# At most three gathers in flight: a wait on the third gather ahead, in a graph attention kernel

## The chip, the core and the metric

The kernel runs on one core of a Trainium2 chip. The metric is the device time of one execution in microseconds. The kernel before took 2567.61 us (median of three runs, 2564.39 to 2570.67). An execution under the hardware profiler is slower: the profiled span is 3156.3 us. Times of single instructions and of waits below come from that profiled execution; the metric is always the time without the profiler.

## The reference

A graph of 3327 nodes has 256 features for each node and a random adjacency matrix in which about 0.48% of the entries are set, some 16 neighbours for each node. Layer 0 is an attention layer in which the score of a neighbour does not depend on the receiving node. Layers 1 to 3 are transformer layers whose attention runs over the neighbours alone:

```
qkv = layer_norm(x, g1, be1) @ w_qkv          # 8 heads of 32
scores = einsum('nhd,mhd->hnm', q, k) * SCALE
scores = where(adj != 0, scores, -inf)
attn = softmax(scores, axis=-1)
out = einsum('hnm,mhd->nhd', attn, v).reshape(n, 256)
x = x + out @ w_proj + b_proj
h2 = layer_norm(x, g2, be2)
x = x + gelu(h2 @ w1 + b1) @ w2 + b2          # 256 -> 1024 -> 256
```

## The kernel before

The first part (up to about 505 us of the profiled span) reads the adjacency matrix, computes layer 0, and turns each row of the matrix into a list of neighbours. The nodes are ranked by their number of neighbours, so that blocks of 128 nodes (there are 26) hold nodes with similar counts. `CAPS` gives the number of neighbour slots of each block, 40 for the first and 10 for the last, 448 in all.

Layers 1 to 3 are run by the class `Layer`. Keys and values of all nodes lie in HBM, one row of 512 floats (528 in layer 1) for each node, in `kv[L]`. For each block and each of its slots, one indirect DMA issued by GpSimd gathers 128 such rows, one for each node of the block, into SBUF: 128 rows of 2 KB, 256 KB for a gather, 448 gathers for a layer, 1344 in all. `issue` (L1288) issues the gathers of one group of up to four slots (`GS = 4`) into one tile of a ring of ten (`NBUF = 10`); the gather itself is L1303. At the start of a layer ten groups are issued; after that one more group is issued each time `values` has read a group and so freed a ring tile. Layer 1 also issues row gathers of `t1` (L1263), and the last layer scatters output rows (L1505), on the same GpSimd queue.

`scores` (L1313) multiplies the keys of a group by the block's queries (L1325) and sums over each head (L1326) on VectorE. After the last group of a block `softmax` runs; some turns later `values` (L1355) weights the values (L1366, VectorE) and adds them up on TensorE with transposes into PSUM (L1372). Projection, layer norm, the feed-forward part and the next layer's q, k and v are cut into small steps, which `some` puts between the groups: matmuls at L1396, L1439, L1462 and L1492, activations at L1445. The keys and values for the next layer are written to HBM by L1500. A layer's gathers need all of these rows, so layers do not overlap in their gathers.

The order on every engine is the order of the calls in the program; a framework layer adds the semaphores. Each DMA that GpSimd issues belongs to one of eight lanes in turn, with a semaphore for each lane, and a DMA waits until the one before it on its lane, which is the eighth ahead, has landed. That is the limit of eight of which the change speaks. The first gather of a group also waits until VectorE (and in layer 1 ScalarE) has read what the ring tile held before.

Of the kernel before, what the change touches and what calls it, by code (L numbers as in the profile page):

```python
# [60 lines left out]
CB = 4  # L61

FAR = 2.0 ** 100


@with_exitstack
# [457 lines left out]
def sparse_path(ctx, tc, ins, out, dram, flag):  # L524
    nc = tc.nc
# [40 lines left out]
    class Norm:  # L566


        def __init__(self, n, name):
            self.n, self.name = n, name  # L570
            self.mv = small.tile([P, 4, 2], FP, tag="mv", name=f"mv_{name}")
# [690 lines left out]
    def gather_rows(b):  # L1262
        nc.gpsimd.indirect_dma_start(  # L1263
            out=t2[:, b, :], out_offset=None, in_=t1,
            in_offset=bass.IndirectOffsetOnAxis(ap=perm[:, b:b + 1].bitcast(U32), axis=0))
# [11 lines left out]
    class Layer:  # L1277
        def __init__(self, L, w, nxt):
            self.L, self.w, self.nxt = L, w, nxt
            self.groups = [g for b in ORDER for g in slots[b]]  # L1280
            self.issued = 0
            self.tiles, self.sc, self.wp, self.q, self.po = {}, {}, {}, {}, {}
            self.rows = 0

            self.short, self.long = [], []
            self.rate = self.credit = 0.0

        def issue(self):  # L1288

            if self.issued == len(self.groups):  # L1290
                return
            L, W = self.L, KVW[self.L]
            b, s0 = self.groups[self.issued]
            self.issued += 1
            while L == 1 and self.rows < min(NB, ORDER.index(b) + 3):
                gather_rows(ORDER[self.rows])
                self.rows += 1
            n = min(GS, CAPS[b] - s0)
            t = ring.tile([P, GS * KVW[1]], FP, tag="kv", name=f"kv_{L}_{b}_{s0}")
            t = t[:, :GS * W].rearrange("p (s c) -> p s c", c=W)  # L1300
            for s in range(n):
                k = 2 * D + s0 + s
                nc.gpsimd.indirect_dma_start(  # L1303
                    out=t[:, s, :], out_offset=None, in_=kv[L],
                    in_offset=bass.IndirectOffsetOnAxis(ap=t2[:, b, k:k + 1].bitcast(U32), axis=0))
            self.tiles[b, s0] = t


# [4 lines left out]
        def scores(self, b, s0):  # L1313
# [4 lines left out]
            if s0 == 0:  # L1318
                self.sc[b] = work.tile([P, LMAX, HEADS], FP, tag="sc", name=f"sc_{L}_{b}")
                if L == 1:  # L1320
                    nc.vector.tensor_scalar(pad[b],
                                            t2[:, b, 2 * D:2 * D + S].bitcast(I32),
                                            0.0, FAR, ALU.is_equal, ALU.mult)
            k = t[:, :n, :D]
# [6 lines left out]
        def softmax(self, b):  # L1331
# [5 lines left out]
            nc.vector.tensor_tensor_reduce(  # L1337
                sc, sc, pad[b][:, :, None].to_broadcast([P, S, HEADS]), 1.0, FAR,
                ALU.add, ALU.min, mx)
# [294 lines left out]
```

## Time and profile before

| | |
|---|---|
| timed, median of three | 2567.61 us |
| profiled span | 3156.3 us |
| VectorE busy | 1935.3 us |
| TensorE matmul busy | 1794.0 us |
| GpSimd busy | 1362.7 us |
| ScalarE busy | 774.6 us |
| gathers, L1303 | 1344, mean 947 ns on GpSimd, 1273.0 us busy |
| data moved by GpSimd's DMAs | 370.26 MB |
| first and last gather start | 509.5 and 3068.0 us |

A line of the profile's groups reads: source line, engine, operation, what is written from what is read, count, then the busy time and the mean of one in ns, then the engine's idle time just before and what ended most of it. "issue" means that the profile shows nothing for which the engine waited; "remote" or "an unknown queue" that what ended the wait is not known. An engine's queue is shown with a q (POOLq is the queue of GpSimd): it decodes, holds waits and dispatches, and can run ahead of the engine. The time of a gather on GpSimd is the time in which its descriptors are made; the data arrive later, which is told by the lane's semaphore.

### The profile page before, as it was taken

To read this page: it belongs to the slowest core of one execution; us is meant where nothing else is said; L and a number is where in the kernel's file an instruction comes from. 1 tells how busy PE (TensorE), PEld (TensorE's weight loads), DVE (VectorE), ACT (ScalarE), POOL (GpSimd) and SP (SyncE) were. 2 spreads that over 40 slices of the span, in tenths; PEclk is the share of its full clock that TensorE was granted. 3 is DMA by queue.
4 is the path that set the end of the run, shared out by engine and by line. 5 is a ranking of instruction groups with operands and counts; after the bars stand their busy time and mean duration, and the time that the engine had idled before them with its cause. 6 is when DMAs were issued, how large, how long until landed. Compare 5 with 4: busy or idle time off the path is not lost.

```text
span 3156.3 us, 24036 instructions
## 1 busy us (share of the span) xinstructions
PE 1794.0 (57%) x7561; PEld 1163.5 (37%) x7561; DVE 1935.3 (61%) x3983; ACT 774.6 (25%) x1316; POOL 1362.7 (43%) x1458
## 2 busy tenths in 40 slices
PE   4767752255666666671457667666713435665556
PEld 3645531133333333350334333433512323433334
DVE  6688995457657656533656756755446556656554
ACT  4455621012222222230112212222300111212112
POOL 4000004545555554305555555544054555565550
PEclk9868766577787886785578778878755766776768
DMA  5334306645555565415455555555064554554560
GB/s 207 131 117 148 129 31 204 174 138 169 165 172 162 156 174 152 112 51 177 141 156 156 163 160 150 175 152 140 24 189 125 156 155 135 169 163 147 161 156 13
DMA packets 144486, 453.80 MB, mean 144 GB/s; under 512 B 29521, under 2 KB 40156, under 8 KB 141021
## 3 DMA queue, kind: packets, MB, share of 16 engines
q0 software_dynamic: 113056, 370.26, 40.9%
q1 hardware_dynamic: 9834, 53.90, 4.9%
q10 hardware_dynamic: 21458, 28.02, 2.5%
q8 instruction: 61, 1.00, 0.1%
q14 instruction: 77, 0.63, 0.1%
HBM read 420.64 MB, written 31.42 MB: 143 GB/s over the span
## 4 chain that ended last, share of the span: by engine, by line
DVE 25%; issue 18%; PE 18%; another core or an unknown queue 17%; POOL 11%; ACT 5%; DMA 5%; DVEq 0%; ACTq 0%; POOLq 0%; SPq 0%
POOL kv L1303 11%; DVE kv L1325 5%; DMA kv<-kv,t 4%; DVE sc L1326 3%; DVE vw L1366 3%; PE pu L1439 3%; PE po L1372 3%; PE py L1462 2%; DVE cand L735 2%; PE pk L1492 1%; PE s_pk L1010 1%; ACT s_aT L724 1%; DVE s_v L731 1%; PE pf L591 1%
## 5 line engine op out<-in xcount | busy, mean ns | idle before, releaser
L1303 POOL DMA_INDIRECT kv<-kv,t x1344 | 1273.0, 947 | 1210.3 <-issue 534.2
L1372 PE MATMUL po<-s_ident,vw 128*128 128x128 f32 x2688 | 475.4, 334 | 580.2 <-DVE vw L1366 387.2
L1372 PEld LDWEIGHTS po<-s_ident,vw 128*128 128x128 f32 x2688 | 395.5, 174 | 724.1 <-issue 373.5
L1325 DVE TENSOR_TENSOR kv<-kv,q 128x1024 f32<-128x1024 f32 (+3 forms) x363 | 413.1, 1138 | 397.1 <-ACT q L1311 274.6
L1366 DVE TENSOR_TENSOR vw<-kv,w 128x1024 f32<-128x1024 f32 x333 | 371.4, 1128 | 87.2 <-remote 84.6
L1326 DVE TENSOR_REDUCE sc<-kv 128x32 f32<-128x1024 f32 (+3 forms) x363 | 414.1, 1141 | 12.4
L1439 PE MATMUL pu<-fT,s_w 128*128 128x512 f32 (+3 forms) x768 | 341.2, 579 | 62.3 <-issue 35.8
L1462 PE MATMUL py<-gT,s_w 128*128 128x512 f32 (+2 forms) x672 | 321.8, 597 | 58.1 <-issue 50.2
L1400 DVE TENSOR_TENSOR t<-t,po 128x256 f32<-128x256 f32 x78 | 32.6, 418 | 390.8 <-remote 254.5
L1445 ACT ACTIVATE gT<-pu,pvb 128x512 f32<-128x512 f32 (+3 forms) x192 | 115.7, 607 | 628.2 <-remote 384.1
L1439 PEld LDWEIGHTS pu<-fT,s_w 128*128 128x128 f32 x768 | 157.4, 222 | 196.1 <-issue 146.4
L1462 PEld LDWEIGHTS py<-gT,s_w 128*128 128x128 f32 x672 | 132.6, 206 | 180.7 <-issue 144.0
L1396 PEld LDWEIGHTS po<-s_w_proj,oT 128*128 128x128 f32 x312 | 71.8, 255 | 281.8 <-issue 272.3
L1394 PE MATMUL po<-bias,s_ones_bf 96*128 96x256 bf16 x78 | 25.2, 324 | 259.7 <-issue 147.4
L1390 ACT COPY oT<-po 128x256 f32<-128x256 f32 x78 | 28.9, 371 | 548.5 <-remote 320.2
L711 POOL MEMSET s_abf<- 128x1 bf16 x23 | 2.2, 104 | 361.4 <-DVE s_v L731 253.7
L1492 PE MATMUL pk<-s_w_qkv,nT 128*128 128x512 f32 x208 | 128.4, 748 | 22.0 <-ACT nT L596 9.9
L735 DVE MAX8 cand<-s_v 128x8 f32<-128x208 bf16 x416 | 118.0, 360 | 0.9
L1396 PE MATMUL po<-s_w_proj,oT 128*128 128x256 f32 x312 | 113.1, 500 | 0.0
L723 PE MATMUL s_ptb<-s_ident_bf,s_abf 128*128 128x128 bf16 x676 | 67.1, 265 | 68.3 <-ACT s_abf L714 45.2
L591 PE MATMUL pf<-s_ident,xn_f 128*128 128x128 f32 x156 | 46.1, 444 | 86.8 <-ACT xn_f L588 66.7
L855 PE MATMUL s_pa<-s_aT,s_hs 128*128 128x256 bf16 x338 | 82.3, 290 | 13.2 <-DVE s_hs L817 13.2
(288 smaller groups left out, 2252.1 us busy)
## 6 DMA issues: line engine op xcount, KB each, us to landing
s_a<-in_adj_dram SPq DMA_DIRECT2D x25, 1663.5 KB
kv<-kv,t POOLq DMA_INDIRECT x1344
kv<-kvr ACTq DMA_DIRECT2D x52, 256.0 KB
kv<-s_kvr ACTq DMA_DIRECT2D x26, 256.0 KB
s_w<-in_L_gnn_w_dram SPq DMA_DIRECT2D x6, 1024.0 KB
t<-ql ACTq DMA_DIRECT2D x6, 592.0 KB
t<-s_x ACTq DMA_DIRECT2D x6, 512.0 KB
s_w_qkv<-in_L_gnn_w_qkv_dram SPq DMA_DIRECT2D x3, 768.0 KB
```

The lines of the kernel that those rows point to most:

```text
L735: nc.vector.max(out=self.cand[:, s, :], in_=self.v[:, s, :])
L855: nc.tensor.matmul(self.pa[:, c0:c0 + 2 * P], S.hs[:r, k, :P], aT[:r, k, :], start=(k == 0), stop=(k == NB - 1))
L1303: nc.gpsimd.indirect_dma_start(out=t[:, s, :], out_offset=None, in_=kv[L], in_offset=bass.IndirectOffsetOnAxis(ap=t2[:, b, k:k + 1].bitcas ...
L1325: nc.vector.tensor_mul(k, k, self.q[b][:, None, :].to_broadcast([P, n, D]))
L1326: nc.vector.tensor_reduce(self.sc[b][:, s0:s0 + n, :], k.rearrange("p s (h d) -> p s h d", d=HD), AX.X, ALU.add)
L1366: nc.vector.tensor_mul(vw[:, :n * D].rearrange("p (s h d) -> p s h d", h=HEADS, d=HD), v, self.wp[b][:, s0:s0 + n, :, None].to_broadcast([ ...
L1372: nc.tensor.matmul(self.po[b][:, k * P:(k + 1) * P], vw[:, at:at + P], ident, is_transpose=True, start=(s0 + s == 0 and k == 0), stop=(s0 ...
L1396: nc.tensor.matmul(ps, c["oT"][:, k * P:(k + 1) * P], w["w_proj"][:, k, :], start=False, stop=(k == 1))
L1439: nc.tensor.matmul(c["pu", f][:, :n], w["w1"][:, e, f * P:(f + 1) * P], c["hT"][:, e, :n], start=(e == 0), stop=(e == 1))
L1445: nc.scalar.activation(g[:, :n], c.pop(("pu", f))[:, :n], AF.Gelu_apprx_tanh, bias=w["b1"][:, f:f + 1])
L1462: nc.tensor.matmul(c["py"][e][:, :n], w["w2"][:, f, e * P:(e + 1) * P], g[:, :n], start=(f == 0), stop=last)
L1492: nc.tensor.matmul(ps[:, :c1 - c0], c["hT"][:, e, j * P:(j + 1) * P], nxt["w_qkv"][:, e, c0:c1], start=(e == 0), stop=(e == 1))
```

## The change

Each gather of a layer, from the fourth on, gets a dependence on the gather three ahead of it: it is not to be issued before that one has landed. The list `flight` holds the gathers of the layer; it is new for each layer, and row gathers and output stores are not in it. The purpose is to keep no more than three gathers in flight, where up to eight could be, so that the DMA engines hold less of a backlog when other transfers come. What is computed, and the order of the instructions, stays.

```diff
+FLIGHT = 3
+WAIT = mybir.DependencyInfo(mybir.DependencyClass.Sync, mybir.DependencyReason.DATA)
...
             self.issued = 0
+            self.flight = []
...
             for s in range(n):
                 k = 2 * D + s0 + s
-                nc.gpsimd.indirect_dma_start(
+                got = nc.gpsimd.indirect_dma_start(
                     out=t[:, s, :], out_offset=None, in_=kv[L],
                     in_offset=bass.IndirectOffsetOnAxis(ap=t2[:, b, k:k + 1].bitcast(U32), axis=0))
+
+                if len(self.flight) >= FLIGHT:
+                    tc.add_manual_dep(got.ins, self.flight[-FLIGHT].ins.name, WAIT,
+                                      reason="gathers in flight")
+                self.flight.append(got)
```

## The prediction

> **What bounds the kernel now.** I read the page first, then the rates of the stages (which engine is busy in which stretch), then the timeline and the chain of waits inside a stretch in which nothing disturbs the work. From the page:
>
> ```profile
> span 3156.3 us, 24036 instructions
> PE 1794.0 (57%) x7561; PEld 1163.5 (37%) x7561; DVE 1935.3 (61%) x3983; ACT 774.6 (25%) x1316; POOL 1362.7 (43%) x1458
> DVE 25%; issue 18%; PE 18%; another core or an unknown queue 17%; POOL 11%; ACT 5%; DMA 5%; DVEq 0%; ACTq 0%; POOLq 0%; SPq 0%
> L1303 POOL DMA_INDIRECT kv<-kv,t x1344 | 1273.0, 947 | 1210.3 <-issue 534.2
> ```
>
> No engine is full, and 17% of the chain, some 540 us, is put down to an unknown queue. The profiled execution takes 3156 us where the timed one takes 2567.61: about 590 us exist only under the profiler, nearly as many as those unexplained waits. So I don't take shares of this span as shares of the timed run; I look for a rate that explains the timed run.
>
> The stretches of the three layers, by the rates of the stages (us; PE, PEld, DVE, ACT, POOL busy; granted clock; DMA share, GB/s):
>
> ```profile
> 505.00:1310.00 805.00, 447.82 (x1580) 267.86 (x1580) 477.34 (x799) 167.52 (x378) 446.88 (x473) 0.73 0.58 168
> 1420.00:2170.00 750.00, 432.24 (x1550) 263.95 (x1549) 468.39 (x764) 157.22 (x266) 407.97 (x431) 0.74 0.53 158
> 2290.00:3070.00 780.00, 377.40 (x1395) 236.38 (x1394) 456.29 (x687) 126.42 (x203) 444.64 (x467) 0.69 0.54 156
> ```
>
> The timeline of GpSimd early in layer 2, where no ring slot is awaited yet:
>
> ```profile
> 1436.91 0.95 POOL L1303 DMA_INDIRECT kv<-kv,t  x1 [0.30 <-issue]
> 1438.16 0.95 POOL L1303 DMA_INDIRECT kv<-kv,t  x1 [0.30 <-issue]
> 1439.41 0.95 POOL L1303 DMA_INDIRECT kv<-kv,t  x1 [0.30 <-issue]
> ```
>
> A gather starts every 1.25 us (0.95 of work, 0.30 between two), never closer. The trace has 471, 448 and 467 GpSimd DMAs from the first gather of a layer to its last (layer 1 has row gathers among them, layer 3 the first output stores). At 1.251 us each that is 589 + 560 + 584 us. First gather of layer 1 at 509.5; 1310.8 to 1428.5 and 2190.8 to 2305.9 pass between layers; 88.3 follow the last gather. Sum: 509.5 + 589 + 117.7 + 560 + 115.1 + 584 + 88.3 = 2564 us, against 2567.61 timed. So the timed run looks like one in which GpSimd issues without a break, and the long idle times are the profiler's. VectorE, with at most 477 us busy in such a layer, keeps up with a group of four gathers each 5.0 us: at a layer's start it waits for landings ("DVE kv L1325 <- DMA kv<-kv,t", 17.7 us of the window from 1428 to 1480). The gathers' pace is the bound.
>
> The chain of waits in the same stretch (start, us, what):
>
> ```profile
> 1436.91 3.56 DMA kv<-kv,t
> 1440.47 0.02 issue
> 1440.49 0.04 POOLq L1303
> ...
> 1446.91 3.66 DMA kv<-kv,t
> 1450.57 0.02 issue
> 1450.59 0.04 POOLq L1303
> ```
>
> The gather that GpSimd started at 1436.91 landed at 1440.47, 3.56 us later, and that released GpSimd's queue, which held the wait of the eighth gather behind it (started 1446.91). So the queue runs some five gathers ahead of the engine, and the limit of eight costs the engine nothing.
>
> **What the Trainium skill says.** "DMA: Bandwidth & Descriptors", Anatomy of one DMA — SWDGE (gpsimd) path: a DMA from GpSimd costs about 2.0 us plus bytes over 436 GB/s, mostly waiting for the receipt of the last write, and a semaphore is waited for before dispatch, not by the DMA engines. For 256 KB that is an estimate of 2.6 us; with 0.95 of descriptor work ahead of it 3.55, and the trace has 3.56 to 3.72. "Perfetto Trace Analysis", DMA Instruction — SWDGE (GPSIMD): the profiled end is the end of descriptor generation, not the landing. The trace agrees: 0.95 us against a landing at 3.6. So the latency that counts here is not the 947 ns of the page. The first of these pages, Latency and other measured facts, gives HBM latency as 0.2 us on average and 2 us at high load: fewer transfers in flight could shorten each. No run here shows that yet.
>
> **The change part by part.** (1) Each of the 1344 gathers but the first three of a layer waits for the third ahead. In the built program the wait for its own lane (the eighth ahead) goes, the wait for a lane three back comes; PE, VectorE, ScalarE and SyncE keep their instructions and waits, and GpSimd gets 24 more instructions that only wait, near the row gathers and layer starts. The trace shows such a wait at 0.04 us: 24 × 0.04 = 1 us, nothing. (2) The limit itself. GpSimd's start of gather k must now follow landing(k-3) plus the time from a release to a start. That delay is in the trace: where VectorE freed a ring slot with GpSimd idle, the start came 0.26 us after (61 cases, median 0.259). The landing semaphores' increments are recorded in part; for the 115 gathers with all 16, start to last increment has quartiles of 3.48, 3.62 and 3.75 us. So the third ahead is ready at 3.62 + 0.26 = 3.88 us after its start, where it used to be given 3 × 1.251 = 3.75. The pace becomes 3.88 / 3 = 1.293 us, 0.042 more per gather: 1344 × 0.042 = 57 us. Behind the waiting gather on GpSimd stand only further gathers, the row gathers and stores; VectorE waits for them.
>
> That is the floor for these latencies, since a late landing delays a gather and an early one gives nothing back. I replayed the three layers with every gather's own landing time (last completion packet of the gather, shifted by 0.33 to meet the 16-increment ones), starts at the later of 1.251 after the previous and 0.26 after landing k-3: 176 us more. Of these some 40 come from bursts: at the start of layer 1 landings take 6 us and at the end of each layer they climb to 9 or 10, because there the DMA engines are full (0.9 busy at 1300 to 1322) and the backlog is the gathers' own; three in flight keep a full DMA engine just as full, so this part is not real. With landings cut off at 4.3 us the replay gives 136. If latencies are 0.1 us shorter in the timed run it is 103, with 0.2 shorter 72, with 0.33 shorter 47. I take 115, between the steady floor and the full replay. (3) The queue can't run five ahead any more; each dispatch waits on a landing. The 0.26 above contains this. (4) Gathers of rows and output stores wait for less than before: some 50 DMAs with 0 to 0.3 us, under 5 us, and not on the path.
>
> **The rivals.** A, the forecast: slower, 2567.6 + 115 = 2683; between +47 and +176 by the bounds above, so 2615 to 2744. B, nothing: the latency without the profiler is below 3.75 - 0.26 = 3.49 us. The skill's 2.6, if it already holds the descriptor work, would do it; then two landed gathers always wait and only rare late ones bind, 2567 to 2573. For it: even now two gathers or fewer are in flight at most starts (1226 of 1344 by the completion packets). Against it: every landing I followed in the chain in undisturbed stretches is 3.5 to 3.7. C, faster: fewer transfers in flight leave the engines to other traffic (instruction fetch, the rows written by L1500, weights), and the unexplained waits of 17% are partly real and shrink. If a tenth of the 540 us is real and half of it goes, 2567.6 - 27 = 2540. For it: PE, ScalarE and VectorE stall together beside dense gathers. Against it: the sum above leaves 3 us for such stalls in the timed run, and in most cases the limit changes nothing of what is in flight, only the timing. D, far slower: the whole 176 plus real bursts, 2760 or more, if a landing's release reaches GpSimd later than VectorE's does; with 0.40 for 0.26, (3.62 + 0.40) / 3 = 1.34, already a floor of 120 us.
>
> **How the numbers follow.** A 0.67, D 0.07, B 0.09, C 0.17. The predicted time is A's, 2683. The range has to take in B (from 2562) and A up to its top; D reaches a little into it: 2562 to 2765. Left out are most of C and a part of D, about 0.2. Faster 0.17, same within 0.2% (5 us) 0.09, slower 0.74.
>
> **What would show it.** In the changed profile gathers that follow each other without a ring wait should start 1.29 to 1.36 us apart, the gap before them 0.34 to 0.41 and no longer a constant 0.30; the idle time before L1303 should be put down to the landing of gathers rather than "issue"; landings should stay near 3.6 us. The 947 ns stay. The profiled span may rise less than the timed one, because there the ring is often full and hides the pace. I am wrong if the gap stays 0.30 (B), or if landings fall below 3.4 with fewer in flight, or if the stalls of PE and ScalarE shrink (C).

## The result, and the profile after

The changed kernel took 2750.85 us (2747.61 to 2752.35), the kernel before, run beside it on the same chip, 2566.99: a ratio of 1.071 (95% interval 1.070 to 1.073), 184 us slower. The forecast was 2683 with a range up to 2765. Its side and its mechanism hold; 68 us of the loss were missing from it. The measured time lies 7 us above the top of the forecast's own bounds (2744) and inside the stated range only because that reached further, towards rival D.

The page after. Its span, 2749.0 us, is now the same as the timed execution:

```profile
span 2749.0 us, 24060 instructions
PE 1696.8 (62%) x7561; PEld 1134.5 (41%) x7561; DVE 1942.6 (71%) x3983; ACT 781.8 (28%) x1316; POOL 1362.2 (50%) x1458
DVE 30%; DMA 25%; PE 19%; issue 11%; POOL 9%; ACT 4%; DVEq 0%; ACTq 0%; SPq 0%; POOLq 0%
L1307 POOL DMA_INDIRECT kv<-kv,t x1344 | 1272.4, 947 | 834.4 <-issue 266.0
kv<-kv,t POOLq DMA_INDIRECT x1344, 3.6
```

The work of a gather on GpSimd, 947 ns, is unchanged, and the busy times of VectorE and ScalarE are within 1% of those before.

The page ahead of the prediction is no fair basis for comparison: it was of a disturbed execution, and in a second profile of the kernel before its 590 us of stalls did not come again. So it doesn't hold either that an execution under the profiler is slower as such: this span, 2568.8 us, goes with a timed run of 2570.72. Page of the kernel before, second profile:

```profile
span 2568.8 us, 24036 instructions
DVE 14%; PE 13%; DMA 13%; POOL 9%; issue 8%; ACT 1%; DVEq 0%; POOLq 0%; SPq 0%; ACTq 0%
L1303 POOL DMA_INDIRECT kv<-kv,t x1344 | 1273.0, 947 | 643.7 <-issue 327.4
```

The shares of the chain that ended last (third line of the page after, second here) settle nothing. DMA has 25% after and had 5% in the first profile before, but here it has 13% of a chain that could be followed through 58% of the span only, and 20% with a limit of six, which costs no time (below). What can be compared are idle times and waits. GpSimd's idle time ahead of gathers rose from 643.7 to 834.4 us, that is by 191. Where it shows on VectorE is told by the waits, before (second profile) and after: engine and line that waited, for what, us in total, times, longest.

```profile
DVE kv L1325 <- DMA kv<-kv,t: 171.7, 105, 8.7
```

```profile
DVE kv L1334 <- DMA kv<-kv,t: 379.6, 180, 8.2
```

VectorE waits 208 us more for landings. It is a follower here: it waits because gathers start later. From the first gather's start of each layer to its last, before: 599.2, 587.6 and 611.0 us, after 678.3, 649.0 and 683.1: 212.6 more. Between the layers and after the last gather 31 us come back (265.4 to 234.2), and the first gather starts 1.2 earlier. 212.6 - 31.2 - 1.2 = 180.2, which is the difference of the two spans.

How the loss comes about is seen in GpSimd's timeline in layer 2 (start, us, what, idle time before it). First the kernel before, second profile, where the gather at 1411.22 is the first of its group and starts 1.25 us after the one ahead, like the others:

```profile
1407.47 0.94 POOL L1303 DMA_INDIRECT kv<-kv,t  x1 [0.30 <-issue]
1408.71 0.95 POOL L1303 DMA_INDIRECT kv<-kv,t  x1 [0.30 <-issue]
1409.96 0.95 POOL L1303 DMA_INDIRECT kv<-kv,t  x1 [0.30 <-issue]
1411.22 0.95 POOL L1303 DMA_INDIRECT kv<-kv,t  x1 [0.30 <-issue]
```

The changed kernel, where 1339.39 and 1344.89 are the first of their groups:

```profile
1339.39 0.94 POOL L1307 DMA_INDIRECT kv<-kv,t  x1 [0.76 <-DMA kv<-kv,t]
1340.64 0.95 POOL L1307 DMA_INDIRECT kv<-kv,t  x1 [0.30 <-issue]
1341.89 0.95 POOL L1307 DMA_INDIRECT kv<-kv,t  x1 [0.30 <-issue]
1343.14 0.95 POOL L1307 DMA_INDIRECT kv<-kv,t  x1 [0.30 <-DMA kv<-kv,t]
1344.89 0.94 POOL L1307 DMA_INDIRECT kv<-kv,t  x1 [0.80 <-DMA kv<-kv,t]
```

and in its chain of waits in the same stretch:

```profile
1340.64 3.51 DMA kv<-kv,t
1344.15 0.02 issue
1344.17 0.02 POOLq L1307
1344.19 0.70 issue
1344.89 3.48 DMA kv<-kv,t
1348.37 0.27 issue
1348.64 0.94 POOL kv L1307
1349.59 0.70 issue
1350.28 3.45 DMA kv<-kv,t
```

Three gathers of four still start 1.25 us after the one ahead of them; the delay falls on one in four. The gather at 1344.89 is the first of a group. The third ahead of it, started at 1340.64, landed at 1344.15, 3.51 us later; then GpSimd's queue did its wait of 0.02, and 0.70 went by before the gather started: 0.74 from landing to start. The gather at 1348.64, the last of its group, started 0.27 after the landing it waited for, at the usual pace. In the built program a gather's own instruction holds one wait. The first gather of a group has two, the landing and VectorE's release of the ring tile, so its landing is awaited in an instruction of its own that only waits, and the gather comes after that. The kernel before has such instructions too: its trace shows 358 at the gathers' line, that of the changed kernel 397 (15 fewer stand at the output stores, so that the program has 24 more).

Over all gathers that waited in the trace after, from landing of the third ahead to start: median 0.259 us for the second to fourth of a group, 0.739 for the first. Of 305 first gathers with more than 0.33 us of idle time ahead, 293 started 0.72 to 0.77 us after that landing. Of the idle time over the constant 0.305 us, first gathers hold 178.7 us, second 11.2, third 28.7, fourth 30.3. The kernel before has 39 in all, waits for ring slots. So the theory that I tested is: the limit of three puts landing and release on the path, as forecast, and **a gather with two waits, of which the one held by the waiting instruction ends late, needs 0.74 us from the end of that wait to its start, not 0.26**, which the queue hid while it could run ahead. Its rivals: the loss is the limit's alone (later landings, spread), or some of it is a cost of extra waits as such, ahead or not.

### The profile page after: what moved, and what is told of

It is laid out like the page before. It is cut to its first block, busy times and chain, and to the rows that moved or that the text cites. A ratio compares the mean times of both kernels' runs of the same rounds, so it can differ in the third digit from the quotient of the medians.

```text
span 2749.0 us, 24060 instructions
## 1 busy us (share of the span) xinstructions
PE 1696.8 (62%) x7561; PEld 1134.5 (41%) x7561; DVE 1942.6 (71%) x3983; ACT 781.8 (28%) x1316; POOL 1362.2 (50%) x1458
## 4 chain that ended last, share of the span: by engine, by line
DVE 30%; DMA 25%; PE 19%; issue 11%; POOL 9%; ACT 4%; DVEq 0%; ACTq 0%; SPq 0%; POOLq 0%
DMA kv<-kv,t 24%; POOL kv L1307 8%; DVE kv L1334 6%; DVE sc L1335 5%; DVE vw L1375 4%; PE pu L1448 4%; PE po L1381 3%; PE py L1471 3%; DVE cand L738 2%; PE s_pk L1013 2%; PE pk L1501 1%; DVE s_v L734 1%; ACT s_aT L727 1%; ACT s_abf L717 1%; DVE st_n L578 1%
## 5 line engine op out<-in xcount | busy, mean ns | idle before, releaser
L1307 POOL DMA_INDIRECT kv<-kv,t x1344 | 1272.4, 947 | 834.4 <-issue 266.0
L1381 PE MATMUL po<-s_ident,vw 128*128 128x128 f32 x2688 | 465.7, 333 | 656.0 <-DVE vw L1375 654.8
L1381 PEld LDWEIGHTS po<-s_ident,vw 128*128 128x128 f32 x2688 | 388.2, 173 | 789.5 <-DVE vw L1375 642.2
L1448 PE MATMUL pu<-fT,s_w 128*128 128x512 f32 (+3 forms) x768 | 326.3, 561 | 6.3 <-ACT gT L1454 3.8
L1471 PE MATMUL py<-gT,s_w 128*128 128x512 f32 (+2 forms) x672 | 286.1, 554 | 0.0
L1501 PE MATMUL pk<-s_w_qkv,nT 128*128 128x512 f32 x208 | 115.6, 683 | 7.2 <-ACT nT L599 7.2
L591 ACT ACTIVATE xn_f<-t,nm_f,rqy_f 128x256 f32<-128x256 f32 x78 | 42.9, 593 | 239.8 <-DVE nm_f L585 233.6
L1349 ACT ACTIVATE sc<-sc,mx 128x120 f32<-128x120 f32 (+6 forms) x78 | 32.0, 410 | 246.8 <-DVE mx L1346 246.3
L1405 PE MATMUL po<-s_w_proj,oT 128*128 128x256 f32 x312 | 100.5, 454 | 0.0
L726 PEld LDWEIGHTS <-s_abf 128*128 128x128 bf16 x676 | 55.2, 120 | 79.4 <-ACT s_abf L717 55.9
L727 ACT COPY s_aT<-s_ptb 128x896 bf16<-128x896 bf16 x104 | 82.2, 860 | 19.3 <-PE s_ptb L726 19.3
```

The lines of the kernel that those rows point to most:

```text
L726: nc.tensor.transpose(pt[:, m, :], self.abf[:, k * P:(k + 1) * P], ident_bf)
L727: nc.scalar.copy(aT[:, k0:k0 + len(ks), :], pt[:, :len(ks), :])
L1307: got = nc.gpsimd.indirect_dma_start(out=t[:, s, :], out_offset=None, in_=kv[L], in_offset=bass.IndirectOffsetOnAxis(ap=t2[:, b, k:k + 1]. ...
L1381: nc.tensor.matmul(self.po[b][:, k * P:(k + 1) * P], vw[:, at:at + P], ident, is_transpose=True, start=(s0 + s == 0 and k == 0), stop=(s0 ...
L1448: nc.tensor.matmul(c["pu", f][:, :n], w["w1"][:, e, f * P:(f + 1) * P], c["hT"][:, e, :n], start=(e == 0), stop=(e == 1))
L1471: nc.tensor.matmul(c["py"][e][:, :n], w["w2"][:, f, e * P:(e + 1) * P], g[:, :n], start=(f == 0), stop=last)
```

## The experiments

**Limits of four, six and two.** The change with another number.

```diff
-FLIGHT = 3
+FLIGHT = 4    # f4;  6 in f6, 2 in f2
```

> The limit at four instead of three. Theory P (the pace is landing plus release over the limit): a gather lands 3.65 us after its start, and the fourth ahead was started 4 x 1.25 = 5.0 us earlier, so even a release that takes 0.74 us is in time; only late landings bind: 2567 to 2600 us. Rival (fewer gathers in flight cost something of themselves, in proportion to what is taken away): four lies between three and eight, so a good part of the 184 us stays: 2690 to 2740 us.

> The limit at six. Theory P: the sixth ahead was started 7.5 us earlier, so that only the late landings at the ends of the layers bind: 2567 to 2573 us, the same as before. Rival (some cost in proportion to what is taken away): 2610 us or more. The profiled span, if a limit below eight alone takes away the long stalls under the profiler, is near 2570 us; if it is the pace of the gathers that does it, some stalls are back.

> The limit at two. Theory P: start is landing of the second ahead plus 0.26 us, or plus 0.74 for the first gather of a group; replayed with the landings of the changed kernel the layers take about 870 us more than with three: 3560 to 3640 us. Rival (fewer in flight make each landing faster, say 3.2 us instead of 3.65): some 0.2 us a gather less, 3300 us.

Measured: limit 4 2585.79 us, 1.006 (1.004 to 1.007) times before; limit 6 2567.71, 1.000 (0.999 to 1.001); limit 2 3421.32, 1.332 (1.330 to 1.334). The small loss with four is clear of noise, though under 1%. With four, a first gather waits for the first of the group before it: median landing 3.71 + 0.74 = 4.45 us against the 5.00 that four issues take, so only late landings bind. With six nothing is left. With two the result falls between the two expectations. The mechanism is there (of the idle time below, three quarters are put to landings), but landings got shorter, median 3.39 us, which I had not put in. The page of limit 2:

```profile
L1307 POOL DMA_INDIRECT kv<-kv,t x1344 | 1271.4, 946 | 1504.2 <-DMA kv<-kv,t 1140.9
kv<-kv,t POOLq DMA_INDIRECT x1344, 3.4
```

**The limit on first gathers alone, and on all others alone.**

```diff
-                if len(self.flight) >= FLIGHT:
+                if s == 0 and len(self.flight) >= FLIGHT:    # first_only;  s > 0 in rest_only
```

> The limit of three on the first gather of each group alone (361 of 1344). Theory T (0.74 us from landing to start for these): nearly the whole loss stays, 2715 to 2740 us. Rival (every gather's wait costs alike): a quarter of 184 us stays, 2613 us.

> The limit of three on all gathers but the first of each group of four (983 of 1344). Theory T (the first gather of a group holds two waits, so its landing wait sits in an instruction of its own and the start follows 0.74 us after the landing, where the others start after 0.26): without these the layers lose about 100 us less, 2645 to 2670 us. Rival (every gather's wait costs alike): three quarters of 184 us stay, 2705 us.

Limiting the first gather of each group alone takes 2744.29 us, 1.068 (1.066 to 1.071): nearly the whole loss from a quarter of the waits (361 of 1344 gathers). Of the 228 that waited, 222 started 0.72 to 1 us after the landing (median 0.765; these hold three waits).

Limiting only the others takes 2700.16, 1.050 (1.049 to 1.052), 30 us above what the theory gave and within 5 us of the rival's 2705. By its time alone this run speaks for the rival; first_only, 131 us above the rival's 2613, speaks against it. The two losses, 173 and 129 us over the kernel before that ran beside them, do not add up to the 184 of the change: a gather that is held up gives those behind it time to become ready. The run is not the clean test that it was meant to be. With first gathers free of the limit, 330 second gathers have to wait for the gather before them on their lane as well, and hold two waits: in the trace 99 of them started 0.26 after the landing, but 66 at 0.72 to 0.76. The cost that I wanted to take away had moved to the next gather.

**The second wait taken off the first gathers.** A tiny memset on GpSimd ahead of a group's first gather awaits the ring tile's release, so most of these gathers are left with the landing alone (waiting instructions at the gathers' line: 66 where the change has 397; the memsets have 333 of their own). 333 memsets of 0.09 us are added, which fit into the 0.30 us between gathers.

```diff
+    tiny = big.tile([1, 1], FP, name="tiny")
...
+            if self.freed:
+                pre = nc.gpsimd.memset(tiny, 0.0)
+                for r in self.freed:      # the reads of the old tile, by VectorE and ScalarE
+                    tc.add_manual_dep(pre.ins, r.ins.name, WAIT, reason="ring tile is free")
...                                # the lines that collect self.freed are left out
```

> The limit of three on all gathers, but the wait for the ring tile is held by a tiny GpSimd memset ahead of the group's first gather (330 of them), so that each gather holds the landing wait alone. Theory T: the start of a group's first gather follows the landing by 0.26 us instead of 0.74; the memset itself takes 0.1 us and a gap; 2665 to 2700 us. Rival (0.74 us has another cause, such as VectorE's release of the tile): the delay stays 0.74 and the time 2750 us or more.

Measured: 2687.23 us, 1.045 (1.043 to 1.047), 64 us under the changed kernel. Timeline of GpSimd:

```profile
1339.37 0.94 POOL L1312 DMA_INDIRECT kv<-kv,t  x1 [0.48 <-DVE t L1416]
1340.30 0.09 POOL L1307 MEMSET tiny<- 1x1 f32 x1
1340.62 0.94 POOL L1312 DMA_INDIRECT kv<-kv,t  x1 [0.23 <-issue]
1341.92 0.95 POOL L1312 DMA_INDIRECT kv<-kv,t  x1 [0.36 <-DMA kv<-kv,t]
```

The first gather, at 1340.62, follows after 1.25 us. Of the 84 first gathers that still waited for a landing 67 started 0.24 to 0.28 after it. Their idle time over 0.305 fell from 178.7 to 32.8 us, while that of third gathers rose from 28.7 to 60.9: a wait taken away in one place is partly paid in the next.

**A second wait put on every gather.** Each gather but the first of a group also waits for a TensorE transpose issued 48 matmuls earlier, one long done; with the limit of three, and with that of eight.

```diff
+                if s > 0 and len(self.mms) > 48:
+                    tc.add_manual_dep(got.ins, self.mms[-48 + s].ins.name, WAIT, reason="second wait")
...                                  # the lines that collect self.mms are left out
-FLIGHT = 3
+FLIGHT = 8    # in two_waits_8 alone
```

> The limit of three, and each gather but the first of a group also waits for a TensorE transpose of about six groups before, long done: every gather now holds two waits. Theory T (two waits put 0.74 us between landing and start, whatever the second one is for): all gathers at 0.74, about 95 us more than the changed kernel, 2820 to 2860 us. Rival (the 0.74 us belongs to the ring tile's release by VectorE): the others stay at 0.26 and the time at 2750 us.

> The same second wait on each gather, but the limit of eight as before. Theory T (the extra instruction costs only when the queue cannot run ahead): 2565 to 2590 us. Rival (instructions that only wait cost by themselves, some 0.2 to 0.5 us for each of about a thousand): 2770 us or more.

With the limit of three: 2812.12 us, 1.095 (1.094 to 1.097), slightly under the range that the theory gave and well above the rival's. Of the gathers that waited for a landing that the trace records, 134 of 139 second, 136 of 151 third and 132 of 142 fourth now started 0.74 after it, where it was 0.259. With the limit of eight: 2567.34, 1.000 (0.999 to 1.001). The same second wait costs nothing when the queue can run ahead, so instructions that only wait don't cost time by being there (the trace with the limit of eight has 1190 of them at the gathers' line). The groups of gathers on the two pages, limit 3 and then 8:

```profile
L1307 POOL DMA_INDIRECT kv<-kv,t x1344 | 1272.1, 947 | 896.2 <-issue 335.7
```

```profile
L1307 POOL DMA_INDIRECT kv<-kv,t x1344 | 1272.7, 947 | 644.0 <-issue 208.2
```

Beside the 834.4 us of the change and the 643.7 of the kernel before, these idle times show the cost, and its absence.

**The kernel before, profiled again.** Nothing edited.

> The kernel before, unchanged, profiled once more. If the long waits for an unknown queue (some 540 us of the profiled span of 3156 us) belong to that one profiled execution, the span is near 2563 us, as with the limit of six and with two waits under the limit of eight; if they belong to the kernel under the profiler, it is near 3150 us again.

Span 2568.8 us, one run 2570.72. The long stalls belonged to the one profiled execution. 784 of 1341 steps between gathers lie at 1.249 to 1.251 us, and 1314 of 1344 gathers have no more than 0.32 us of idle time ahead of them, so GpSimd's pace is what bounds the kernel before.

**All together.** From the start of a group's first gather to that of the next group, median over 279 groups of four (the first ones of each layer left out), beside what landing (median of that trace), pace, and the time from the end of the wait to the start (0.74 or 0.26) give:

| kernel | working | us | measured us |
|---|---|---|---|
| before | 4 × 1.25 | 5.00 | 5.00 |
| limit 4 | first after first: 3.71 + 0.74 = 4.45, under 4 × 1.25 | 5.00 | 5.00 |
| limit 3, the change | 3.65 + 0.74 + one step of 1.25 | 5.64 | 5.67 |
| limit 3, first gathers alone | 3.66 + 0.765 + one step of 1.25 | 5.68 | 5.68 |
| limit 3, memset ahead | 4/3 × (3.68 + 0.26) | 5.25 | 5.36 |
| limit 3, two waits on all | 4/3 × (3.62 + 0.74) | 5.81 | 5.79 |
| limit 2 | (3.39 + 0.74) + (3.39 + 0.26) | 7.78 | 7.75 |

The limit on all but the first gathers, 5.43 us measured, is left out, since its wait moved among the gathers. The third row is the case of the chain shown above: the first gather waits for the second of the group before, which started one step after that group's first. 0.67 us more for each of 309 groups of four is 207 us, beside the 212.6 that the three layers grew by. The memset row is the one that reads low: with 0.26 the median landing leaves little to wait (3.94 against 3.75), so that landings later than the median count for more. Drawing landings at random from that trace, with 0.26 for each gather, gives an estimate of 5.48 for the median and 5.74 for the mean; measured are 5.36 and 5.71.

## Why the prediction was right, and where it was short

**The bound: right, its sum partly by luck.** GpSimd's pace of 1.251 us bounds the kernel before. But the sum of 2564 us came out through two errors that cancel. The layers' gathers take 1797.8 us (second profile), not 589 + 560 + 584 = 1733: ring slots cost 39 us of it, and in layer 3 the 19 output stores between the gathers took 51 us with the idle time ahead of them, where 24 had been counted. The boundaries and the end take 265.4, not 321, which had been read from the disturbed execution.

**The change of the limit, (2): right for gathers with one wait.** Landing and release of the third ahead set the start of many gathers, and 0.26 from landing to start is what 18 of 20, 52 of 58 and 96 of 105 of the second, third and fourth gathers that waited show. The landing of 3.62 is near: 3.65 in the trace after. The replay's cut of the landings at 4.3 us was near as well: for the last 18 gathers of a layer the median landing was 5.8 to 7.5 us before and is 4.3 to 4.5 with three in flight, and those gathers idle only 5.7 us a layer over the constant.

**"The 0.26 above contains this", (3): the step that failed.** The dispatch on a landing costs 0.26 for a gather with one wait and 0.74 for one with two. The 0.26 had been read where VectorE's release ended the wait; there the landing had long been awaited in the instruction ahead, and only the last of the two waits was seen. In the changed kernel the first of the two is the late one. Item (1) had put the waiting instructions at 0.04 us each and looked at the 24 added ones; the ones that matter were in the program before, and their cost lies in the 0.70 us after them. The runs size it: with 0.26 for most first gathers too (the memset) the loss is 116 us over the kernel before that ran beside it, against the 115 that were taken; the other 68 of the change's 184 are what the second wait adds. That 116 meets 115 so closely is partly luck: 115 was picked between 57 and 176, and some first gathers of that run still waited 0.74.

**The rivals.** B, nothing: refuted. Landings under the profiler are as long as the timed runs need them to be, since spans and times agree within 0.1% after. C, stalls that shrink: refuted by the second profile, which has none to take back. D, far slower: its stated reason, a landing's release that reaches GpSimd later than VectorE's, holds for the gathers with two waits and for no others, and the time came within 10 us of its 2760, nearer than to A's 2683. D had been given a chance of 0.07. That the stated range holds the result is to that extent luck.

**What would show it.** Forecast were gaps of 0.34 to 0.41 between gathers; in fact 833 of 1335 stay at about 0.30 and the loss gathers at the groups' first. By the forecast's own text an unchanged 0.30 spoke for B, so a reader of the median gap alone would have decided wrongly. The idle time was to be put to landings instead of "issue". From the waits of the trace after:

```profile
POOL kv L1307 <- issue: 266.0, 777, 3.2
POOL kv L1307 <- DMA kv<-kv,t: 232.1, 373, 3.1
```

Most of the first line, 207.5 us, is the constant 0.30 ahead of 681 second to fourth gathers. And of the 305 first gathers with more than 0.33 us ahead of them only 85 are put to a landing, 162 to instructions of VectorE. The semaphore by which VectorE tells of the release is raised by 3134 of its instructions, and where one of them ended between the landing and the start, as in all these 162, the view names that one. The delay from landing to start tells more than the name. The span was to rise less than the time under the profiler; against the second profile it rose by 180, the time by 184. Landings stayed near 3.6, as forecast. "DMA: Bandwidth & Descriptors" of the Trainium skill (Latency and other measured facts) had suggested shorter latencies at lower load; the runs show a little of it, a median of 3.74 before, 3.65 with three in flight and 3.39 with two.

**Left open.** Why the gather needs 0.70 us after a waiting instruction isn't seen, nor whether the order of the two waits matters: in each of these kernels it was the landing that was awaited first, and the reverse wasn't tried. What the 31 us between the layers and at the end came from wasn't traced. TensorE's granted clock was a little lower in the slower kernel (0.778 in the second profile before, 0.766 after), and its matmuls were busy for 1678.0 and 1696.8 us; no run holds the clock fixed, but the start of 293 of 305 delayed first gathers at a set time after a landing leaves it little room. No version was found that beats the kernel before; limits of six and eight equal it.

## What to carry to other kernels

A limit of n transfers in flight costs little as long as n times the pace of issue is more than the landing plus the time from the end of the wait to the start; here 4 × 1.25 passes and costs 0.6%, by late landings, 6 × 1.25 costs nothing, and 3 × 1.25 doesn't pass. Size that time for the instruction that will wait, by its number of waits, and not by a delay that is in the trace for another kind of wait. A queue that runs ahead hides such costs, and an added wait that stops it from running ahead shows them all at once, those of old waits included. And profile a kernel twice before its stalls are taken for its own: here 590 us of them belonged to one execution.

## What the runs showed of the hardware

- A gather on GpSimd with one wait started 0.259 us after the landing that released it; one with two, the landing awaited first in an instruction of its own, 0.739, of which 0.70 lie between that instruction's end and the gather's start.
- Landing of 128 rows of 2 KB, from the gather's start: median over the recorded landings 3.74 us in the kernel before, 3.71 with at most four in flight, 3.65 with three, 3.39 with two.
- The 0.70 us after a waiting instruction cost nothing where GpSimd's queue could run ahead: a second wait on every gather left the time at 2567.34 us with a limit of eight, and took it to 2812.12 with a limit of three.
- Of two profiled executions of the same kernel one took 3156.3 us, with some 540 put to an unknown queue, and one 2568.8.
